# Second attention of a gated cross-attention network: both heads' maxima turned in one tile, masked queries made by ScalarE, order planned anew

## The chip, the cores and the metric

The kernel runs on one core of a Trainium2 chip. The metric is the device time of one execution in microseconds, as the median of several runs. A core has five engines that work side by side, each through its own queue of instructions in order: TensorE (PE, matrix products and transposes, results in PSUM), VectorE (DVE), ScalarE (ACT), GpSimd (POOL) and SyncE (SP, which issues DMAs). Semaphores order them. PSUM has eight banks of 2 KB per partition.

## The reference

For `x` of 8 batches x 256 rows x 256 columns and a context of 8 x 120 x 128:

```text
x = x + tanh(g_xattn[0]) * attention0(layernorm(x), ctx)          # one head
x = x + tanh(g_ffn[0])   * experts(layernorm(x))                  # 8 experts + 4 pass-through, top 2
x = x + tanh(g_xattn[1]) * attention1(layernorm(x), ctx)          # 16 heads of 16
x = x + tanh(g_ffn[1])   * fp8_linear(layernorm(x))               # fp8-rounded weights and inputs
```

The change is in `attention1`:

```text
qh, kh, vh = heads(q @ Wq + bq), heads(k @ Wk + bk), heads(v @ Wv + bv)   # 16 heads of width 16
scores = einsum('bhqd,bhkd->bhqk', qh, kh) / 4
out    = concat(softmax(scores) @ vh) @ Wo + bo
```

A softmax needs each row's maximum taken off before the exponential.

## The kernel before

The program runs in four stages: the first attention with the routing tables (to about 85 us), the blocks of the experts (to about 196 us, and PE then has a branch until 203.9), the second attention (to about 320 us), and the fp8 layer. Within a stage an order written out as text sets each engine's queue: every word is an "atom", a small function that records a few instructions, and each engine takes its own instructions in the order of the words. `ORDER1` is that text for the second attention; `AHEAD` puts the work of batches 0 to 2 that can go early beside the expert blocks. A planner wrote these orders offline; nothing is reordered on the chip.

The second attention works in 16 steps k = (batch b, half ec). A half has 128 of the 256 query columns, which are 8 heads in four "quarters" of 32 partitions (`QR`) with two heads each. Its atoms are:

| atom | engine | what it does (line) |
|---|---|---|
| G.b.c.k | POOL | fetches rows of the experts' results (L1193) |
| cb.b.c | DVE | adds two of them into x (L1203) |
| nf, vf, of; pf | DVE; POOL | moments, variance, offset (L1211 to L1225); power -1/2 (L1220) |
| ap.b.c; tx, xe | ACT; PE, ACT | normalises (L1230); turns x (L1244), copies it out (L1250) |
| q.b, qe.b | PE, ACT | query projection (L1256), out of PSUM with its bias (L1265) |
| gb.b | POOL | adds the output bias to x (L1272) |
| m.k | PE | scores by rows: 8 products of 32 rows, into two PSUM pairs (L1285) |
| r.k.i | DVE | negated maxima over the 120 keys, of pair i, into `mpad` (L1300) |
| p.k | PE | turns `mpad` (L1309) |
| d.k | DVE | puts the turned maxima beside the masked queries (L1319), two instructions |
| w.k | PE | scores by columns, less the maxima, 8 products into two pairs (L1332) |
| e.k.i | ACT | exponential (L1340) |
| o.k, f.k | PE, ACT | product with the values (L1352), copied out (L1359) |
| t.k, c.k, a.k, g.k | PE, DVE, PE, ACT | turned (L1367), divided by the sums (L1373, L1376), turned back (L1386), copied out (L1392) |
| P.b, x.b | PE, DVE | output projection (L1398), added to x (L1405) |
| nb, vb, pb, ob, an, am | DVE, POOL, ACT | the next layer norm (L1230 too), and the largest magnitude (L1412) |

A number after `*` puts that many warm-up matmuls before an atom of PE (L1172). PSUM holds three `pair` tiles of two banks each, taken in turn by m and w (two a step), and two tiles of one bank, `one`, taken in turn by tx, q, p, o, t, a and P. A tile can be written again when whatever read it last has done so.

How a maximum is taken off: `kz` holds, for each quarter, the keys with all rows but one head's set to zero, so a product over 32 rows gives one head's scores. `kq` is the same with a row of ones added in the other head's first row. If the query operand carries the negated maximum in that row, the product comes out with the maximum taken off. `pmask` has two columns, 1 in the rows of head 0 or of head 1 of each quarter. `mpad` is 5 x 128 columns wide; r writes one head's maxima at an offset of 16 and the other's at 0, so that after a transpose for each head and half of the rows (four) each maximum lies in the right row, with zeros elsewhere. d then computes qT x pmask + pm for each of the two heads.

Of the kernel before, what the change touches and what calls it, by code (L numbers as in the profile page):

```python
# [67 lines left out]
ORDER1 = """
m.0 q.2 r.0.0 G.4.0.0 r.0.1 G.4.0.1 m.1 qe.2 cb.3.0 G.4.1.0 p.0 r.1.0 G.4.1.1 d.0 m.2 G.5.0.0
r.1.1 r.2.0 G.5.0.1 p.1*1 d.1 w.0 G.5.1.0 r.2.1 e.0.0 G.5.1.1 cb.3.1 p.2*1 e.0.1 w.1 G.6.0.0 d.2  # L70
o.0 nf.3.0 e.1.0 G.6.0.1 cb.4.0 e.1.1 m.3 G.6.1.0 nf.3.1 f.0 vf.3 o.1 r.3.0 G.6.1.1 t.0 f.1 r.3.1
w.2 pf.3 G.7.0.0 of.3 p.3 c.0 e.2.0 d.3 a.0 G.7.0.1 e.2.1 m.4 cb.4.1 g.0 G.7.1.0 t.1 ap.3.0 r.4.0
o.2 ap.3.1 gb.3 c.1 w.3 f.2 r.4.1 G.7.1.1 a.1 e.3.0 tx.3 nf.4.0 xe.3 m.5 nf.4.1 g.1 vf.4 e.3.1
cb.5.0 pf.4 p.4 q.3 of.4 d.4 ap.4.0 ap.4.1 r.5.0 gb.4 o.3 qe.3 r.5.1 P.0 f.3 nf.5.0 cb.5.1 p.5 x.0
w.4 d.5 t.2 e.4.0 nb.0.0 t.3 c.2 e.4.1 w.5 c.3 a.2 e.5.0 nb.0.1 o.4 vb.0 nf.5.1 pb.0 g.2 m.6 e.5.1
vf.5 pf.5 ob.0 cb.6.0 a.3 f.4 g.3 r.6.0 o.5 an.0.0 an.0.1 P.1 of.5 r.6.1 f.5 ap.5.0 am.0 ap.5.1
p.6 x.1 gb.5 m.7 d.6 tx.4 r.7.0 t.4 xe.4 c.4 q.4 nb.1.0 r.7.1 a.4 qe.4 w.6 cb.6.1 g.4 p.7 nb.1.1
e.6.0 t.5 d.7 e.6.1 m.8 c.5 o.6 r.8.0 a.5 f.6 r.8.1 w.7 g.5 vb.1 p.8 cb.7.0 e.7.0 pb.1 P.2 ob.1
e.7.1 d.8 an.1.0 nf.6.0 o.7 an.1.1 x.2 w.8 nb.2.0 f.7 nb.2.1 t.6 e.8.0 vb.2 t.7 pb.2 c.6 e.8.1 m.9
c.7 ob.2 a.6 r.9.0 an.2.0 o.8 g.6 an.2.1 tx.5 r.9.1 f.8 xe.5 am.1 p.9 q.5 d.9 cb.7.1 w.9 qe.5  # L80
nf.6.1 vf.6 t.8 nf.7.0 pf.6 e.9.0 a.7 c.8 g.7 m.10 of.6 e.9.1 nf.7.1 a.8 vf.7 ap.6.0 r.10.0 pf.7
o.9 g.8 ap.6.1 P.3 of.7 r.10.1 f.9 gb.6 ap.7.0 am.2 ap.7.1 p.10 x.3 gb.7 m.11 d.10 tx.6 nb.3.0 t.9
xe.6 r.11.0 q.6 c.9 r.11.1 a.9 qe.6 w.10 nb.3.1 g.9 vb.3 p.11 pb.3 e.10.0 P.4 d.11 e.10.1 ob.3
an.3.0 o.10 x.4 an.3.1 w.11 nb.4.0 f.10 am.3 t.10 e.11.0 nb.4.1 tx.7 c.10 e.11.1 m.12 vb.4 pb.4
xe.7 o.11 r.12.0 a.10 f.11 r.12.1 m.13 g.10 ob.4 p.12 an.4.0 r.13.0 q.7 an.4.1 d.12 am.4 w.12 qe.7
r.13.1 t.11 e.12.0 p.13 c.11 e.12.1 m.14 d.13 a.11 r.14.0 o.12 g.11 P.5 r.14.1 f.12 t.12 x.5 w.13
c.12 nb.5.0 e.13.0 a.12 p.14 nb.5.1 e.13.1 m.15 d.14 g.12 vb.5 pb.5 r.15.0 o.13 r.15.1 f.13 w.14
ob.5 t.13 e.14.0 p.15 c.13 e.14.1 d.15 a.13 g.13 w.15 an.5.0 an.5.1 o.14 e.15.0 am.5 P.6 f.14
e.15.1 o.15 x.6 nb.6.0 t.14 f.15 c.14 t.15 c.15 a.14 g.14 nb.6.1 a.15 vb.6 g.15 pb.6 P.7*1 ob.6
an.6.0 an.6.1 x.7 nb.7.0 nb.7.1 vb.7 am.6 pb.7 ob.7 an.7.0 an.7.1 am.7  # L90
"""
# [7 lines left out]
def flamingo_gated(ctx: ExitStack, tc: tile.TileContext, a: dict, out: bass.AP):  # L99
    nc = tc.nc  # L100
# [1191 lines left out]
    def at_r1(k, i):  # L1292

        sc = held["m", k][i]

# [4 lines left out]
        nc.vector.tensor_reduce(  # L1300
            m[:, :, :, :, 0], sc[:, :, : 4 * SK].rearrange("p r (c h k) -> p r c h k", c=TB, h=2),
            AX.X, ALU.max, negate=True,
        )

    def at_p1(k, warmed):
        pm = held["p", k] = one(f"pm_{k}", warmed, (P, 2, TB * P))
        for h in range(2):
            for c in range(TB):
                nc.tensor.transpose(  # L1309
                    pm[:, h, c * P : (c + 1) * P], mpad[k % 2][:, (2 * c + h) * P :][:, :P], ident  # L1310
                )

    def at_d1(k):

        b, ec = steps[k]
        pm = held.pop(("p", k))
        turned[k] = att1.tile([P, 2, TB * P], F32, tag="qm", name=f"qm_{k}")
        for h in range(2):
            nc.vector.scalar_tensor_tensor(  # L1319
                turned[k][:, h, :], qT[b][:, ec, :], pmask[:, h : h + 1], pm[:, h, :],  # L1320
                ALU.mult, ALU.add,
            )

# [287 lines left out]
```

## Time and profile before

| what | value |
|---|---|
| median of 3 runs | 346.2 us (346.15 to 348.18) |
| profiled execution | 349.1 us |
| its span, first to last instruction | 347.4 us |
| PE busy | 302.6 us, 87% (weight loads 233.3 us, 67%) |
| DVE busy | 237.7 us, 68% |
| ACT busy | 168.0 us, 48% |
| POOL busy | 117.7 us, 34% |
| mean granted TensorE clock | 0.919 |

The profile has the busy time of each engine, the same in stretches of time, groups of instructions by line (busy time, mean of one, and the idle time just before them with what ended it), and a timeline. The mean of one instruction is from its start to its end. Matmuls overlap in PE's pipeline, so the time that one holds PE is read from its start to the start of the next. The profiled execution has its own time, which is not one of the three runs.

### The profile page before, as it was taken

How to read it: one execution, taken by the hardware profiler on the slowest of the kernel's cores; microseconds unless marked ns; L12 is line 12 of the kernel's file. 1: busy time of each engine (PE TensorE's matmuls, PEld its weight loads, DVE VectorE, ACT ScalarE, POOL GpSimd, SP SyncE). 2: the span in 40 equal slices, each digit the busy share in tenths (PEclk: the TensorE clock that was granted, in tenths of full speed). 3: DMA queues.
4: the chain of work that ended last, by engine and by line, in shares of the span. 5: the costliest groups of instructions: out<-in, count | busy, mean ns of one | idle time of the engine just before them, and what ended most of it. 6: DMA issues, size and time to landing. Idle time of an engine off the chain costs nothing. (4 is left out here: it accounts for less than half of the span.)

```text
span 347.4 us, 6779 instructions
## 1 busy us (share of the span) xinstructions
PE 302.6 (87%) x2284; PEld 233.3 (67%) x2284; DVE 237.7 (68%) x714; ACT 168.0 (48%) x331; POOL 117.7 (34%) x165
## 2 busy tenths in 40 slices
...
GB/s 124 285 277 323 123 124 0 2 0 242 256 219 218 187 217 198 215 252 183 256 260 45 107 37 93 94 30 2 2 0 2 4 0 2 3 0 0 2 60 181
DMA packets 26518, 40.18 MB, mean 116 GB/s; under 512 B 4432, under 2 KB 13744, under 8 KB 26480
## 3 DMA queue, kind: packets, MB, share of 16 engines
...
q14 instruction: 16, 0.13, 0.1%
...
## 5 line engine op out<-in xcount | busy, mean ns | idle before, releaser
L1109 PEld LDWEIGHTS bh<-xbT,w 128*128 128x128 f32 x416 | 50.1, 192 | 2.5 <-DVE xbT L1103 1.1
L1109 PE MATMUL bh<-xbT,w 128*128 128x128 f32 x416 | 50.9, 276 | 0.5 <-DVE xbT L1103 0.5
L1120 PE MATMUL by<-w,hidT 128*128 x208 | 49.0, 379 | 0.0
L1300 DVE TENSOR_REDUCE mpad<-sc 128x8 f32<-128x960 f32 x32 | 36.0, 1150 | 14.5 <-PE sc L1285 14.5
L1103 DVE COPY xbT<-bx 128x256 f32<-128x256 f32 x26 | 11.0, 422 | 47.0 <-PE bx L1101 46.8
L1078 POOL DMA_INDIRECT xb<-rows,from_i x26 | 26.8, 1031 | 47.3 <-PE bx L1101 39.4
L1120 PEld LDWEIGHTS by<-w,hidT 128*128 128x128 f32 x208 | 37.6, 190 | 4.1
L1340 ACT ACTIVATE es<-st 120x1024 f32<-120x1024 f32 x32 | 31.5, 1024 | 14.3 <-PE st L1332 10.3
L1193 POOL DMA_INDIRECT y<-made,back x32 | 32.3, 1010 | 14.1 <-issue 13.6
L1114 ACT ACTIVATE hidT<-bh 128x512 f32<-128x512 f32 x26 | 15.5, 597 | 39.3 <-PE bh L1109 36.6
L1220 POOL TENSOR_TENSOR rsd<-ved,mhalf 128x2 f32<-128x2 f32 x8 | 5.7, 715 | 59.9 <-DVE ved L1216 59.9
L1285 PE MATMUL sc<-kz,qT 32*128 32x240 f32 x256 | 21.2, 404 | 5.0 <-PEq L1460 5.0
L1126 ACT COPY yb<-by 128x256 f32<-128x256 f32 x26 | 9.7, 372 | 32.2 <-PE by L1120 31.8
L1285 PEld LDWEIGHTS sc<-kz,qT 32*128 32x128 f32 x256 | 14.2, 192 | 9.5 <-issue 8.5
L1256 PE MATMUL pq<-xT,wq 128*128 128x256 f32 x64 | 17.3, 418 | 1.8 <-ACT xT L1250 1.8
L1332 PE MATMUL st<-qm,kq 32*120 32x256 f32 x256 | 18.6, 398 | 0.2 <-DMA y<-made,back 0.2
L1265 ACT ACTIVATE qT<-pq,bq 128x256 f32<-128x256 f32 x16 | 6.7, 471 | 22.3 <-PE pq L1256 12.6
L1352 PE MATMUL vo<-es,v 120*32 120x256 f32 x256 | 17.1, 385 | 0.1
L1256 PEld LDWEIGHTS pq<-xT,wq 128*128 128x128 f32 x64 | 12.6, 207 | 5.0 <-ACT xT L1250 2.8
L1398 PE MATMUL po<-wo,cT 128*128 128x256 f32 x64 | 15.7, 388 | 0.0
L1203 DVE SCALAR_TENSOR_TENSOR x<-y,share,x 128x256 f32<-128x256 f32 x32 | 15.3, 477 | 0.6
L1220 POOL TENSOR_TENSOR rsc<-vec,mhalf 128x2 f32<-128x2 f32 x8 | 5.7, 718 | 28.8 <-DVE vec L1216 28.5
...
## 6 DMA issues: line engine op xcount, KB each, us to landing
...
```

The lines of the kernel that those rows point to most:

```text
L1078: nc.gpsimd.indirect_dma_start(out=xb[j % NX].bitcast(I32), out_offset=None, in_=rows, in_offset=bass.IndirectOffsetOnAxis(ap=from_i[:, j ...
L1109: nc.tensor.matmul(ph[:, f, :], w1[j % NW][:, dc, f * P : (f + 1) * P], xbT[j][:, dc, :], start=(dc == 0), stop=(dc == DC - 1),)
L1114: nc.scalar.activation(hidT[j], ph, AF.Silu)
L1120: nc.tensor.matmul(py, hidT[j][:, f, :], w2[:, bass.ds(e, 1), f * D : (f + 1) * D].rearrange("p o d -> p (o d)"), start=(f == 0), stop=(f ...
L1193: nc.gpsimd.indirect_dma_start(out=y.bitcast(I32), out_offset=None, in_=made[:n, :], in_offset=bass.IndirectOffsetOnAxis(ap=back_i[:, b * ...
L1256: nc.tensor.matmul(pq[:, ec, :], wq1[:, dc, ec * P : (ec + 1) * P], xq_[b][:, dc, :], start=(dc == 0), stop=(dc == DC - 1),)
L1285: nc.tensor.matmul(held["m", k][r // 2][:, r % 2, c * 2 * SK : (c + 1) * 2 * SK], qT[b][rows_, ec, c * P : (c + 1) * P], kz[rows_, b, ec, ...
L1300: nc.vector.tensor_reduce(m[:, :, :, :, 0], sc[:, :, : 4 * SK].rearrange("p r (c h k) -> p r c h k", c=TB, h=2), AX.X, ALU.max, negate=True,)
L1332: nc.tensor.matmul(st[r // 2][:SK, r % 2, h * TB * P : (h + 1) * TB * P], kq[rows_, b, ec, h, :], qm[rows_, h, :], start=True, stop=True,)
L1340: nc.scalar.activation(weighed[k][:, 2 * i : 2 * i + 2], held["w", k][i][:SK].rearrange("p r (h t) -> p r h t", h=2), AF.Exp, scale=1.0 / ...
L1352: nc.tensor.matmul(vo[r * QR : (r + 1) * QR, h, :], v1[:, b, ec * HC + 2 * r + h, :], es[:, r, h, :], start=True, stop=True,)
L1398: nc.tensor.matmul(po[:, c, :], cT[b][:, dc, c * P : (c + 1) * P], wo1[:, dc, :], start=(dc == 0), stop=(dc == DC - 1),)
```

## The change

- r writes both heads' maxima of a quarter into one tile of 128 rows and columns for each half of the query rows: column 32r + 16h of `mpad`, now 2 x 128 columns wide. p turns it with two transposes, not four, and its result has half the size.
- After this transpose, the two heads' maxima of a quarter lie in one tile, so d multiplies the turned maxima by the mask and adds queries that are masked already: pm x pmask[1 - h] + qz[h].
- The masked queries `qz` are made by a new atom z.b on ACT, two multiplications of 128 x 512 for each batch, into a new tile with two buffers of 4 KB per partition each.
- For a maximum to land in the other head's row, `kz` has its two heads in exchanged order.
- `wk`, `wv` and `ctxT` (some 8 KB per partition) move from a pool that lives all through the kernel to one of the first attention.
- ORDER1 is written anew, with the z atoms in it and without the warm-ups before p.1 and p.2. `AHEAD`, ORDER and ORDER2 stay.

```diff
 ORDER1 = """
-m.0 q.2 r.0.0 G.4.0.0 r.0.1 G.4.0.1 m.1 qe.2 cb.3.0 G.4.1.0 p.0 r.1.0 G.4.1.1 d.0 m.2 G.5.0.0
-r.1.1 r.2.0 G.5.0.1 p.1*1 d.1 w.0 G.5.1.0 r.2.1 e.0.0 G.5.1.1 cb.3.1 p.2*1 e.0.1 w.1 G.6.0.0 d.2
-o.0 nf.3.0 e.1.0 G.6.0.1 cb.4.0 e.1.1 m.3 G.6.1.0 nf.3.1 f.0 vf.3 o.1 r.3.0 G.6.1.1 t.0 f.1 r.3.1
-w.2 pf.3 G.7.0.0 of.3 p.3 c.0 e.2.0 d.3 a.0 G.7.0.1 e.2.1 m.4 cb.4.1 g.0 G.7.1.0 t.1 ap.3.0 r.4.0
-o.2 ap.3.1 gb.3 c.1 w.3 f.2 r.4.1 G.7.1.1 a.1 e.3.0 tx.3 nf.4.0 xe.3 m.5 nf.4.1 g.1 vf.4 e.3.1
-cb.5.0 pf.4 p.4 q.3 of.4 d.4 ap.4.0 ap.4.1 r.5.0 gb.4 o.3 qe.3 r.5.1 P.0 f.3 nf.5.0 cb.5.1 p.5 x.0
-w.4 d.5 t.2 e.4.0 nb.0.0 t.3 c.2 e.4.1 w.5 c.3 a.2 e.5.0 nb.0.1 o.4 vb.0 nf.5.1 pb.0 g.2 m.6 e.5.1
-vf.5 pf.5 ob.0 cb.6.0 a.3 f.4 g.3 r.6.0 o.5 an.0.0 an.0.1 P.1 of.5 r.6.1 f.5 ap.5.0 am.0 ap.5.1
-p.6 x.1 gb.5 m.7 d.6 tx.4 r.7.0 t.4 xe.4 c.4 q.4 nb.1.0 r.7.1 a.4 qe.4 w.6 cb.6.1 g.4 p.7 nb.1.1
-e.6.0 t.5 d.7 e.6.1 m.8 c.5 o.6 r.8.0 a.5 f.6 r.8.1 w.7 g.5 vb.1 p.8 cb.7.0 e.7.0 pb.1 P.2 ob.1
-e.7.1 d.8 an.1.0 nf.6.0 o.7 an.1.1 x.2 w.8 nb.2.0 f.7 nb.2.1 t.6 e.8.0 vb.2 t.7 pb.2 c.6 e.8.1 m.9
-c.7 ob.2 a.6 r.9.0 an.2.0 o.8 g.6 an.2.1 tx.5 r.9.1 f.8 xe.5 am.1 p.9 q.5 d.9 cb.7.1 w.9 qe.5
...
+m.0 z.0 q.2 z.1 r.0.0 G.4.0.0 r.0.1 G.4.0.1 m.1 qe.2 cb.3.0 G.4.1.0 p.0 cb.3.1 d.0 G.4.1.1 r.1.0
+G.5.0.0 r.1.1 w.0 G.5.0.1 nf.3.0 p.1 e.0.0 nf.3.1 G.5.1.0 d.1 e.0.1 m.2 vf.3 cb.4.0 G.5.1.1 z.2
+o.0 r.2.0 G.6.0.0 f.0 r.2.1 w.1 pf.3 cb.4.1 t.0 e.1.0 G.6.0.1 p.2 of.3 c.0 e.1.1 m.3 G.6.1.0 d.2
+ap.3.0 cb.5.0 o.1 ap.3.1 G.6.1.1 r.3.0 tx.3 f.1 gb.3 xe.3 r.3.1 a.0 w.2 g.0 cb.5.1 G.7.0.0 q.3
+e.2.0 nf.4.0 G.7.0.1 nf.4.1 e.2.1 vf.4 nf.5.0 p.3 G.7.1.0 qe.3 m.4 nf.5.1 d.3 G.7.1.1 o.2 r.4.0
+z.3 t.1 pf.4 r.4.1 f.2 m.5 of.4 c.1 ap.4.0 t.2 ap.4.1 r.5.0 a.1 gb.4 g.1 c.2 w.3 vf.5 r.5.1 pf.5
+a.2 e.3.0 P.0 of.5 cb.6.0 ap.5.0 g.2 cb.6.1 e.3.1 p.4 m.6 x.0 ap.5.1 d.4 gb.5 p.5 r.6.0 o.3 d.5
+w.4 f.3 nb.0.0 t.3 r.6.1 e.4.0 tx.4 e.4.1 c.3 w.5 nb.0.1 xe.4 p.6 vb.0 cb.7.0 e.5.0 pb.0 q.4
+cb.7.1 e.5.1 ob.0 d.6 an.0.0 m.7 qe.4 nf.6.0 a.3 nf.6.1 an.0.1 o.4 g.3 r.7.0 z.4 o.5 vf.6 am.0
+pf.6 f.4 w.6 r.7.1 f.5 t.4 of.6 e.6.0 nf.7.0 p.7 c.4 e.6.1 m.8 d.7 ap.6.0 nf.7.1 a.4 ap.6.1 o.6
+vf.7 r.8.0 pf.7 g.4 tx.5 gb.6 f.6 of.7 r.8.1 w.7 xe.5 ap.7.0 q.5 e.7.0 e.7.1 p.8 m.9 qe.5 d.8 z.5
+o.7 r.9.0 ap.7.1 t.5 r.9.1 gb.7 w.8 f.7 c.5 p.9 e.8.0 P.1 d.9 e.8.1 a.5 x.1 w.9 g.5 nb.1.0 P.2
+nb.1.1 e.9.0 vb.1 pb.1 e.9.1 ob.1 t.6 x.2 an.1.0 m.10 an.1.1 c.6 nb.2.0 a.6 t.7 r.10.0 g.6 tx.6
+c.7 m.11 xe.6 r.10.1 a.7 q.6 r.11.0 g.7 r.11.1 P.3 nb.2.1 qe.6 vb.2 am.1 pb.2 z.6 ob.2 p.10 x.3
+an.2.0 m.12 an.2.1 d.10 o.8 am.2 nb.3.0 o.9 f.8 nb.3.1 t.8 vb.3 r.12.0 f.9 pb.3 p.11 c.8 w.10 d.11
+a.8 e.10.0 r.12.1 t.9 g.8 c.9 w.11 e.10.1 ob.3 a.9 an.3.0 o.10 g.9 e.11.0 P.4 f.10 e.11.1 p.12 x.4
...
-    mpad = [near.tile([P, 5 * P], F32, name=f"mpad_{i}", bufs=1) for i in range(2)]
+    mpad = [near.tile([P, TB * P], F32, name=f"mpad_{i}", bufs=1) for i in range(2)]
...
-            nc.vector.tensor_scalar(kz[:, bs, ec, h, :], src, pmask[:, h : h + 1], None, ALU.mult)
+            nc.vector.tensor_scalar(kz[:, bs, ec, 1 - h, :], src, pmask[:, h : h + 1], None, ALU.mult)
...
-        at = DK + 2 * i * QR
-        m = mpad[k % 2][:, at : at + 4 * P].rearrange("p (c s) -> p c s", c=TB)
-        m = m[:, :, : 2 * (P - DK)].rearrange("p c (h s) -> p c h s", h=2)
-        m = m[:, :, :, : 2 * QR].rearrange("p c h (r s) -> p r c h s", r=2)
+        m = mpad[k % 2].rearrange("p (c i r h s) -> p i r c h s", c=TB, i=2, r=2, h=2)[:, i]
...
     def at_p1(k, warmed):
-        pm = held["p", k] = one(f"pm_{k}", warmed, (P, 2, TB * P))
-        for h in range(2):
-            for c in range(TB):
-                nc.tensor.transpose(
-                    pm[:, h, c * P : (c + 1) * P], mpad[k % 2][:, (2 * c + h) * P :][:, :P], ident
-                )
+        pm = held["p", k] = one(f"pm_{k}", warmed, (P, TB * P))
+        for c in range(TB):
+            cs = slice(c * P, (c + 1) * P)
+            nc.tensor.transpose(pm[:, cs], mpad[k % 2][:, cs], ident)
+
+    def at_z1(b):
+
+        qz[b] = att1.tile([P, 2, DC, TB * P], F32, tag="qz", name=f"qz_{b}")
+        for h in range(2):
+            nc.scalar.mul(qz[b][:, h], qT[b], pmask[:, h : h + 1])
...
-                turned[k][:, h, :], qT[b][:, ec, :], pmask[:, h : h + 1], pm[:, h, :],
+                turned[k][:, h, :], pm, pmask[:, 1 - h : 2 - h], qz[b][:, h, ec, :],
                 ALU.mult, ALU.add,
```

More of the change, by code (lines that the diff above doesn't have):

```diff
@@ L80 @@
-c.7 ob.2 a.6 r.9.0 an.2.0 o.8 g.6 an.2.1 tx.5 r.9.1 f.8 xe.5 am.1 p.9 q.5 d.9 cb.7.1 w.9 qe.5
[L81 to L90, printed above, removed]
+m.0 z.0 q.2 z.1 r.0.0 G.4.0.0 r.0.1 G.4.0.1 m.1 qe.2 cb.3.0 G.4.1.0 p.0 cb.3.1 d.0 G.4.1.1 r.1.0
@@ new lines @@
+c.7 m.11 xe.6 r.10.1 a.7 q.6 r.11.0 g.7 r.11.1 P.3 nb.2.1 qe.6 vb.2 am.1 pb.2 z.6 ob.2 p.10 x.3
+an.2.0 m.12 an.2.1 d.10 o.8 am.2 nb.3.0 o.9 f.8 nb.3.1 t.8 vb.3 r.12.0 f.9 pb.3 p.11 c.8 w.10 d.11
+a.8 e.10.0 r.12.1 t.9 g.8 c.9 w.11 e.10.1 ob.3 a.9 an.3.0 o.10 g.9 e.11.0 P.4 f.10 e.11.1 p.12 x.4
+an.3.1 m.13 d.12 tx.7 nb.4.0 o.11 xe.7 nb.4.1 vb.4 q.7 am.3 pb.4 f.11 r.13.0 ob.4 r.13.1 an.4.0
+w.12 qe.7 p.13 an.4.1 t.10 d.13 e.12.0 c.10 t.11 e.12.1 m.14 am.4 c.11 z.7 a.10 r.14.0 o.12 g.10
+r.14.1 a.11 f.12 w.13 g.11 p.14 e.13.0 P.5 d.14 e.13.1 t.12 x.5 m.15 c.12 nb.5.0 a.12 o.13 r.15.0
@@ L91 @@
+g.12 r.15.1 f.13 w.14 nb.5.1 t.13 e.14.0 vb.5 p.15 pb.5 c.13 e.14.1 d.15 a.13 g.13 ob.5 w.15
+an.5.0 an.5.1 P.6 e.15.0 am.5 e.15.1 o.14 x.6 nb.6.0 o.15 f.14 nb.6.1 t.14 vb.6 f.15 pb.6 c.14
+t.15 ob.6 a.14 c.15 an.6.0 g.14 a.15 an.6.1 g.15 am.6 P.7*1 x.7 nb.7.0 nb.7.1 vb.7 pb.7 ob.7
+an.7.0 an.7.1 am.7
 """
@@ L157, in load_row @@
         engine.dma_start(out=t, in_=a[key].partition_broadcast(t.shape[0]))
-    wk = res.tile([P, 2, D], F32, name="wk")
-    wv = res.tile([P, 2, D], F32, name="wv")
-    ctxT = res.tile([P, B * SK], F32, name="ctxT")
+    wk = att0.tile([P, 2, D], F32, name="wk", bufs=1)
+    wv = att0.tile([P, 2, D], F32, name="wv", bufs=1)
+    ctxT = att0.tile([P, B * SK], F32, name="ctxT", bufs=1)
     def load_kv(t, i, key):
@@ L1158, in flamingo_gated @@
     amax = const.tile([P, B + 1], F32, name="amax")
-    mpad = [near.tile([P, 5 * P], F32, name=f"mpad_{i}", bufs=1) for i in range(2)]
-    xq_, qT, cT, back_rows, rstd, off, mv = {}, {}, {}, {}, {}, {}, {}
+    mpad = [near.tile([P, TB * P], F32, name=f"mpad_{i}", bufs=1) for i in range(2)]
+    xq_, qT, qz, cT, back_rows, rstd, off, mv = {}, {}, {}, {}, {}, {}, {}, {}
     held, turned, weighed, summed, cats = {}, {}, {}, {}, {}
```

4 lines of the change are left out of this document (2 added, 2 removed).

## The prediction

> **What bounds the kernel now.** I read the busy time by stretches first. The change sits in the second attention, which runs from about 204 to 315 us.
>
> ```profile
> core 0: us, PE busy (x) PEld busy (x) DVE busy (x) ACT busy (x) POOL busy (x), PEclk, DMA share, GB/s
> ...
> 215.00:240.00 25.00, 24.50 (x277) 16.27 (x273) 23.44 (x59) 16.68 (x24) 12.46 (x14) 1.00 0.18 51
> 240.00:260.00 20.00, 19.76 (x211) 13.49 (x204) 18.62 (x45) 12.71 (x24) 3.42 (x4) 1.00 0.00 1
> 260.00:280.00 20.00, 19.45 (x182) 14.06 (x182) 16.98 (x45) 12.60 (x23) 5.33 (x6) 1.00 0.01 2
> 280.00:300.00 20.00, 20.00 (x210) 13.90 (x212) 16.48 (x38) 12.26 (x20) 0.69 (x1) 1.00 0.00 1
> ```
>
> PE looks full everywhere. DVE is at 94% (23.44 of 25) and 93% up to 260 us, and at 85% and 82% after it. So there are two bounds, and they change places near 260 us. To see what one piece of PE work really costs, I went to the timeline.
>
> ```profile
> 264.36 0.63 PE L1309 MATMUL pm<-ident,mpad 128*128 128x128 f32 x4 [0.31 <-DVE mpad L1300]
> ...
> 264.83 1.90 PE L1256 MATMUL pq<-xT,wq 128*128 128x256 f32 x8
> 265.03 0.87 DVE L1319 SCALAR_TENSOR_TENSOR qm<-qT,pmask,pm 128x256 f32<-128x256 f32 x2 [0.22 <-PE pm L1309]
> ...
> 266.66 1.14 PE L1332 MATMUL st<-qm,kq 32*120 32x256 f32 x16
> ...
> 267.73 0.66 PE L1367 MATMUL vt<-ident,vs 128*128 128x128 f32 x4
> ...
> 269.92 0.44 PE L1386 MATMUL ct<-ident,cat 128*128 128x128 f32 x2
> ...
> 270.29 1.07 PE L1352 MATMUL vo<-es,v 120*32 120x256 f32 x16
> ...
> 271.29 1.99 PE L1398 MATMUL po<-wo,cT 128*128 128x256 f32 x8
> ```
>
> Durations overlap here; what counts is start to next start. Four transposes (pm) hold PE for 264.83 - 264.36 = 0.47 us, two (ct) for 270.29 - 269.92 = 0.37, vo for 1.00, st for 1.07, pq for 1.83. Over the stage the typical paces are m 1.02, p 0.51, w 1.07, o 1.00, t 0.51, a 0.33 per step, and P 1.83, q 1.83, tx 0.51 per batch: 16 x 4.44 + 8 x 1.83 + 6 x 1.83 + 5 x 0.51 = 99.2 us. The stage takes 110.9 (m.0 starts at 203.9, P.7 ends at 314.8). The other 11.7 us: 2.6 go to m.0 and q.2, which run at half pace after PE's idle branch, the rest is waiting.
>
> ```profile
> L1340 ACT ACTIVATE es<-st 120x1024 f32<-120x1024 f32 x32 | 31.5, 1024 | 14.3 <-PE st L1332 10.3 <-issue 3.9
> L1300 DVE TENSOR_REDUCE mpad<-sc 128x8 f32<-128x960 f32 x27 | 30.4, 1150 | 0.8 <-PE sc L1285 0.8
> L1319 DVE SCALAR_TENSOR_TENSOR qm<-qT,pmask,pm 128x256 f32<-128x256 f32 x29 | 12.6, 474 | 2.2 <-PE pm L1309 2.2
> L1309 PE MATMUL pm<-ident,mpad 128*128 128x128 f32 x56 | 8.8, 280 | 0.7 <-DVE mpad L1300 0.7
> ```
>
> These groups are of the stretch from 215 to 320 us. The maxima (L1300) are the largest DVE row and waited for PE just 0.8 us: DVE is the one that is waited for.
>
> **The change, part by part.** *Two transposes fewer a step.* p drops from four to two, so from 0.51 to about 0.31 (the ct row is the same shape twice): 16 x 0.20 = 3.2 us less PE work, 99.2 to 96.0. Which duration counts matters: the Trainium skill ("TensorE: Matmul & The Clock Gate", Part 4) gives about 275 ns for such a transpose in a kernel, and the L1309 row agrees with a mean of 280. By that, 32 x 0.28 = 9 us would go. The starts, 0.11 us apart inside a group, say the mean is mostly pipeline; I take 3.2.
>
> *ACT makes the masked queries.* z is two multiplications of 128x512 a batch by a column. The nearest row is the same form:
>
> ```profile
> L1063 ACT ACTIVATE qm_w<-wf,s_w 128x512 f32<-128x512 f32 x1 | 0.7, 725 | 0.0
> ```
>
> With about 0.1 us overlap, 1.27 us a batch, 8 x 1.27 = 10.2 us; ACT's queue grows from 62 to 72 us of a 111 us stage. z.0 and z.1 stand ahead of qe.2, where ACT now idles for 9.7 us; z.2 stands ahead of f.0, z.4 ahead of f.4, z.7 ahead of g.10. Behind each I find 1 us or more before PE wants the result. Cost 0; without that cover 1.3 us each for z.4 and z.7, the two with least.
>
> *The combining step d* keeps two DVE instructions of one shape; the PSUM operand changes places. L1203, same operation all from SBUF, takes 478 against 474: 0. *r* writes the same 128x8 with other strides: 0. *Clearing mpad* shrinks (2 x 592 ns for 640 columns, now 256), at 141 us, where DVE is under half busy: 0. *wk, wv, ctxT in another pool*: kz's first write (102 us) now waits also for loads that landed before 70 us: 0. POOL's power pf.3 passes three gathers; gathers go out 1.3 us apart, land in 3.1, and are wanted over 5 us after that: 0.
>
> *The two warm-up matmuls* before p.1 and p.2 (0.4 us each) lay in waits of 1.1 us: 0. What they guard is the granted clock, the column after the engines:
>
> ```profile
> 204.00:209.00 5.00, 5.00 (x24) 3.69 (x24) 3.01 (x4) 0.00 (x0) 3.16 (x4) 0.50 0.19 56
> 209.00:214.00 5.00, 4.50 (x43) 2.65 (x41) 3.61 (x6) 2.12 (x3) 3.96 (x4) 0.99 0.37 105
> ```
>
> It was 0.50 after PE's branch of 4.2 us and stayed up over the waits of 1.1 us. The skill (same page, Part 1) puts the limit at some 3.4 us idle; I expect no wait over 1.5 us. If the clock were lost once, 3.4 us at half pace cost 1.7.
>
> *The new order.* This decides. DVE's total is unchanged, but its queue is not. Paces from the trace: r 1.07, d 0.79 a pair, cb 0.92, nf and nb 0.58, c 0.68, x 0.67, am 0.60, small ones 0.09. Summed along each queue, without waits: DVE to the end of d.k, PE to the start of w.k, which needs d.k.
>
> ```text
> k               3     4     7     9    11    15
> before  DVE  16.5  23.3  42.7  54.9  67.6  87.4
>         PE   16.5  25.1  43.0  54.7  69.9  90.8
> after   DVE  21.7  30.9  44.6  51.9  68.0  87.3
>         PE   19.9  25.8  39.2  48.5  65.3  87.6
> ```
>
> DVE counts from 205.95, PE from 203.9 + 2.6 = 206.5. Before, the two keep step. After, cb.3 to cb.7 and nf.3 to nf.6 (10 and 9 pieces against 8 and 6) stand ahead of d.7: DVE is about 5 us late at w.4 and w.7. Up to there PE's saving is worth nothing, as PE waits for DVE. This is also what the skill's "Perfetto Trace Analysis" (Identifying the Most-Contended Engine) says against the change: matmul busy time is no measure of headroom, LDWEIGHTS busy is. PEld is 65 to 70% in the windows above, DVE 94%. By that rule the gain is 0; by the PE row, where starts follow each other without a gap, it is 3.2. The queue sums say: 0 until about w.7, partly after.
>
> The second half of w.7 also needs the PSUM pair that r.8.0 frees (three pairs in turn). r.8.0 ends at 46.3 in the new DVE queue. Walking the head of both queues by hand gives 0.9 us of DVE idle before that. The same walk of the old queue from r.1.0 (210.47) to d.4 gives 19.5 us, the trace 20.4, so I add 0.8 for small waits: 205.95 + 46.3 + 0.9 + 0.8 = 254.0. w.7 ends 0.8 later, at 254.8; before it ended at 255.45. **-0.65.** What is left for PE after w.7 is 96.0 - 40.3 = 55.7, before 99.2 - 44.0 = 55.2: more, as P.1, P.2 and others now come later. **+0.5.** Waits after w.7 were 314.8 - 255.45 - 55.2 = 4.2. In the new order I walk two more: o.8, o.9 and p.11 follow each other through two one-bank tiles (x.3, d.10, f.9 must free them), and the first half of w.11 waits for r.12.1. Together some 1 to 1.5 over what it had. **+1.2.** Sum: **+1.0 us**. The tail and the FFN keep their order of dependence: 0.
>
> The profiled execution took 349.1 us, 347.4 of it span; the median shown is 2.9 lower. The difference carries over: 346.2 + 1.0 = **347.2 us**. A measurement tells about 1% (3.5 us) from no change, so this counts as the same.
>
> **Rivals.** *A wash* as summed (chance 0.57): 347.2, own range 344.7 to 349.6.
>
> *PE's saving comes through* (0.18): if DVE's waits inside the head vanish and PE is the bound from w.1 on, 346.2 - 3.2 = 343.0, at best half a us less. For it: PE starts follow without a gap from 218 us on. Against it: the table, and DVE at 94%.
>
> *DVE idles in its own head* (0.25): slower. The three pairs make a loop: m.5's second half waits for r.4.0, r.5.0 for m.5, w.3's second half for r.5.0, and so on to d.7. As DVE is the late one there, each us that it idles before d.7 passes whole to the end. In the trace it idled 252.4 - 205.95 - 42.7 = 3.8 us up to d.7; I counted 1.7. The old figure again gives +2.1; the loop closing four times at about 0.5 us of handing over gives 2 more, less what the later waits then absorb: 350.0. It decides from 4.2 us of idle on. For it: d.3 comes at 21.7 against 16.5. Against it: DVE has cb and nf pieces ready in these places.
>
> That transposes are not removed can be left out: the order of PE's queue shows two pm in each step.
>
> **Numbers.** Of the wash nearly all lies within 1%; of the PE case a bit over half is beyond 1% faster (0.11), of the DVE case most beyond 1% slower (0.20), with 0.02 on either side for the wash's edges. Faster 0.13, same 0.65, slower 0.22. The range from 342.7 to 350.6 holds the first two cases with the late clock or uncovered z (1.3 to 1.7), and most of the third.
>
> **What will show it.** pm x2 at about 0.3 us from start to start; z of 0.72 us; DVE over 94% busy from 215 to 255; w.3 starting near 232.5 (before 226.9), w.4 near 238.5 (before 235.8), w.7 within 1.5 us of 254; w.11 near 281; P.7 ending near 316. If w.4 is on time, the table fails; if w.7 starts after 257, the DVE rival is right; if P.7 ends before 313, PE was the bound.

## The result and the profile after

The changed kernel took **349.0 us** (median; 347.2 to 350.2) against 346.8 us for the kernel before on the same chip: a ratio of **1.0051, 95% interval 1.0032 to 1.0070**, so 1.8 us more (1.1 to 2.4). Predicted was +1.0.

Some runs of a kernel are over 1.5% above its fastest; the ratios leave these out, and the one profile of experiment 10 is of such a run. The traces also differ outside the changed stage. The first gather of the experts falls anywhere from 81.0 to 86.3 us, with a granted clock of 0.97 to 0.85 up to 80 us. The end after P.7 takes one of two lengths, about 31.6 or 32.5: 32.5 in both traces of before and in experiment 4, the shorter one in after and in all others. So the two profiled spans, 347.4 before and 347.3 after, are no comparison. I compare what lies between: from the end of PE's branch to the end of P.7. (The branch ends at 203.41 us before and 201.47 after.)

| us | before | before, run again | after |
|---|---|---|---|
| end of the branch to m.0 | 0.47 | 0.47 | 2.40 |
| m.0 to end of w.7 | 51.65 | 51.85 | 50.47 |
| end of w.7 to end of P.7 | 59.37 | 59.37 | 61.36 |
| sum: branch to P.7 | 111.48 | 111.69 | 114.24 |

The sum grows by 2.6 to 2.8. With the end, which is 0.9 shorter in after's trace, that is 1.7 to 1.9. The busy time by stretches, after:

```profile
core 0: us, PE busy (x) PEld busy (x) DVE busy (x) ACT busy (x) POOL busy (x), PEclk, DMA share, GB/s
...
204.00:209.00 5.00, 5.00 (x32) 3.57 (x36) 3.01 (x4) 1.87 (x4) 3.78 (x5) 0.62 0.30 85
209.00:214.00 5.00, 3.42 (x38) 1.99 (x32) 4.62 (x10) 2.73 (x4) 3.78 (x5) 1.00 0.32 98
...
215.00:240.00 25.00, 23.17 (x242) 14.56 (x238) 24.51 (x55) 16.25 (x27) 13.20 (x13) 1.00 0.15 44
240.00:260.00 20.00, 19.81 (x226) 13.19 (x222) 18.14 (x44) 18.27 (x30) 4.16 (x5) 1.00 0.01 2
260.00:280.00 20.00, 19.67 (x177) 13.92 (x173) 17.17 (x44) 11.41 (x19) 2.67 (x4) 1.00 0.01 2
280.00:300.00 20.00, 18.97 (x188) 12.73 (x186) 13.64 (x32) 14.76 (x24) 0.69 (x1) 1.00 0.00 1
```

In the head (215 to 240) DVE went from 94 to 98% and PE fell to 93%: PE waits for DVE there. From 240 to 260 three engines are full at once, PE 99%, ACT 91%, DVE 91%; before, ACT was at 64% there. PE has holes again from 280 to 300.

The groups of 215 to 320 us (busy time, mean ns of one | idle time before, with what ended it):

```profile
L1299 DVE TENSOR_REDUCE mpad<-sc 128x8 f32<-128x960 f32 x28 | 31.4, 1147 | 0.1
...
L1322 DVE SCALAR_TENSOR_TENSOR qm<-pm,pmask,qz 128x256 f32<-128x256 f32 x29 | 12.6, 476 | 3.0 <-PE pm L1308 2.9
...
L1314 ACT ACTIVATE qz<-qT,pmask 128x512 f32<-128x512 f32 x12 | 8.0, 718 | 1.4 <-DVE qm L1322 1.2
...
L1308 PE MATMUL pm<-ident,mpad 128*128 128x128 f32 x28 | 5.7, 284 | 0.1
```

The single prices came out as taken: r with its new strides 1147 ns (1150), d 476 (474), z 718 (725), a transpose 284 in the mean. And on PE's timeline after:

```profile
273.65 0.38 PE L1308 MATMUL pm<-ident,mpad 128*128 128x128 f32 x2
273.96 1.09 PE L1286 MATMUL sc<-kz,qT 32*128 32x240 f32 x16
...
278.18 1.83 PE L1335 MATMUL st<-qm,kq 32*120 32x256 f32 x16
279.94 0.44 PE L1389 MATMUL ct<-ident,cat 128*128 128x128 f32 x2
280.45 0.63 PE L1370 MATMUL vt<-ident,vs 128*128 128x128 f32 x4
281.42 1.14 PE L1335 MATMUL st<-qm,kq 32*120 32x256 f32 x16 [0.34 <-DVE mpad L1299]
```

Two transposes hold PE 273.96 - 273.65 = 0.31 us, as against 0.47 for four. But w.10 (278.18) takes 1.76 to the next start where 1.07 is its pace, t.9 (280.45) 0.97 instead of about 0.5, and w.11 waits in the open: the late place that the prediction named.

What it did not name is at the start of the stage. In the first listing ACT and PE after, in the second ACT and PE before:

```profile
202.37 0.72 ACT L1314 ACTIVATE qz<-qT,pmask 128x512 f32<-128x512 f32 x1 [7.22 <-DMA y<-made,back]
203.00 0.82 ACT L1266 ACTIVATE qT<-pq,bq 128x256 f32<-128x256 f32 x2
...
203.87 1.98 PE L1286 MATMUL sc<-kz,qT 32*128 32x240 f32 x16 [6.67 <-ACT qT L1266]
```

```profile
198.95 0.84 ACT L1265 ACTIVATE qT<-pq,bq 128x256 f32<-128x256 f32 x2 [2.08 <-PE pq L1256]
...
203.88 1.98 PE L1285 MATMUL sc<-kz,qT 32*128 32x240 f32 x16 [4.96 <-PEq L1460]
```

The first half of z.0 stands in ACT's queue ahead of qe.1 (the copy of batch 1's queries out of PSUM, which AHEAD puts beside the experts). z.0 is the first write into the pool `att1`, whose memory held other things until the experts ended; so it waits for all of them, to 202.37, nearly a microsecond after PE's branch ended (201.47). ACT takes nine semaphore waits one after the other for it, from 201.67 to 202.33; the listing names the last releaser only. qe.1 follows at 203.00 instead of before the branch, and m.0 needs the PSUM bank that qe.1 frees. Before, m.0 waits for PE's own branch alone (PEq L1460).

### The profile page after: what moved, and what is told of

It reads as the page before. It is cut to its first block, busy times and chain, and to the rows that moved or that the text cites. A ratio compares the mean times of both kernels' runs of the same rounds, so it can differ in the third digit from the quotient of the medians.

```text
span 347.3 us, 6721 instructions
## 1 busy us (share of the span) xinstructions
PE 298.3 (86%) x2250; PEld 228.2 (66%) x2250; DVE 238.9 (69%) x714; ACT 178.6 (51%) x347; POOL 118.2 (34%) x165
## 5 line engine op out<-in xcount | busy, mean ns | idle before, releaser
L1299 DVE TENSOR_REDUCE mpad<-sc 128x8 f32<-128x960 f32 x32 | 35.9, 1147 | 14.1 <-PE sc L1286 14.0
L1194 POOL DMA_INDIRECT y<-made,back x32 | 32.4, 1012 | 14.1 <-issue 13.5
L1286 PE MATMUL sc<-kz,qT 32*128 32x240 f32 x256 | 19.7, 403 | 6.7 <-ACT qT L1266 6.7
L1335 PE MATMUL st<-qm,kq 32*120 32x256 f32 x256 | 22.0, 402 | 3.2 <-DVE mpad L1299 2.4
L1286 PEld LDWEIGHTS sc<-kz,qT 32*128 32x128 f32 x256 | 13.0, 192 | 10.3 <-ACT qT L1266 7.1
L1335 PEld LDWEIGHTS st<-qm,kq 32*120 32x120 f32 x256 | 12.9, 177 | 9.7 <-issue 4.0
L326 PE MATMUL warm<-every 128*128 128x512 bf16 x44 | 15.5, 502 | 1.1 <-DVE every L232 1.1
L1204 DVE SCALAR_TENSOR_TENSOR x<-y,share,x 128x256 f32<-128x256 f32 x32 | 16.0, 508 | 0.6
L1322 DVE SCALAR_TENSOR_TENSOR qm<-pm,pmask,qz 128x256 f32<-128x256 f32 x32 | 13.9, 476 | 3.4 <-PE pm L1308 3.2
```

What stands on the lines that cost most here:

```text
L1194: nc.gpsimd.indirect_dma_start(out=y.bitcast(I32), out_offset=None, in_=made[:n, :], in_offset=bass.IndirectOffsetOnAxis(ap=back_i[:, b * ...
L1204: nc.vector.scalar_tensor_tensor(x, back_rows.pop((b, c, k)), share[:, b * TB + c, k : k + 1], x, ALU.mult, ALU.add)
L1286: nc.tensor.matmul(held["m", k][r // 2][:, r % 2, c * 2 * SK : (c + 1) * 2 * SK], qT[b][rows_, ec, c * P : (c + 1) * P], kz[rows_, b, ec, ...
L1299: nc.vector.tensor_reduce(m[..., 0], sc[:, :, : 4 * SK].rearrange("p r (c h k) -> p r c h k", c=TB, h=2), AX.X, ALU.max, negate=True,)
L1335: nc.tensor.matmul(st[r // 2][:SK, r % 2, h * TB * P : (h + 1) * TB * P], kq[rows_, b, ec, h, :], qm[rows_, h, :], start=True, stop=True,)
```

## The experiments

Times of kernels are told as ratios to the kernel before on the same chip. Where the trace is compared, the measure is the one above, from the branch's end to P.7's end: 111.5 to 111.7 before, 114.24 after.

**1. z.0 and z.1 behind qe.2.**

```diff
-m.0 z.0 q.2 z.1 r.0.0 ... m.1 qe.2 cb.3.0
+m.0 q.2 r.0.0 ... m.1 qe.2 z.0 z.1 cb.3.0
```

> The changed kernel with z.0 and z.1 moved behind qe.2. Theory A (z.0 is the first instruction that writes the new pool, waits there for PE's branch, and holds up the copy of q.1 behind it on ACT, whose PSUM bank m.0 needs): m.0 starts 0.4 to 0.6 us after PE's branch ends, in place of 2.4; d.0 may wait up to 0.5 us for z.0; the time falls by 1.3 to 2 us, ratio to the kernel before about 1.000. Theory B (all of the loss lies in the new order's waits inside the stage): gap or no gap, the time stays at a ratio of 1.005.

Measured: 349.45 us, ratio 1.0062 (1.0033 to 1.0090). m.0 came 0.47 after the branch, so the hold-up is gone; branch to P.7 is 113.18, 1.06 less than after, not 1.93. About half of the gain went elsewhere: q.2 ran longer at half clock (3.54 us to m.1's start, 2.88 after), and w.1's second half waited 1.07 us for the maxima, not 0.86. The expected ratio of about 1.000 was missed: the median shows nothing of the gain.

**2. qz in a pool that is open already.**

```diff
-        qz[b] = att1.tile([P, 2, DC, TB * P], F32, tag="qz", name=f"qz_{b}")
+        qz[b] = near.tile([P, 2, DC, TB * P], F32, tag="qz", name=f"qz_{b}")
```

> The changed kernel with the masked queries in a pool that is open already in the expert stage, so that z.0 has nothing of the closed pools to wait for; the order is the changed kernel's. Theory A: the wait, not the place in the text, is what costs; m.0 starts 0.4 to 0.6 us after the branch, the stage from m.0 to P.7 stays at 111 to 112 us, the ratio falls to 0.999 to 1.001. Theory B: no change, 1.005. If m.0 is on time in the other run and late here, it is the place on ACT and not the wait.

Measured: 348.37 us, ratio 1.0046 (1.0025 to 1.0068); branch to m.0 0.47, branch to P.7 112.96. On ACT and PE in this kernel:

```profile
198.38 0.84 ACT L1266 ACTIVATE qT<-pq,bq 128x256 f32<-128x256 f32 x2 [2.08 <-PE pq L1257]
199.25 1.33 ACT L1314 ACTIVATE qz<-qT,pmask 128x512 f32<-128x512 f32 x2
...
203.14 1.98 PE L1286 MATMUL sc<-kz,qT 32*128 32x240 f32 x16 [4.80 <-PEq L1463]
```

The text of the order is untouched; only the memory differs. In ACT's queue qe.1 now comes ahead of z.0, z.0 runs before the branch ends, and m.0 waits for the branch alone. Eight of the semaphore waits, for the same semaphores, now stand ahead of the first exponential (208.76 to 209.34 us), which is ACT's first write into `att1` here. So the pool, not the work of z, held m.0 up: it brings both the wait and the place ahead of qe.1. It is worth 114.24 - 112.96 = 1.3 us in the trace. The medians do not confirm this price: 1.3 us less than after would be a ratio of 1.0014, below the interval of this kernel and of experiment 1, and the expected 0.999 to 1.001 was missed. This kernel is the base for experiments 8, 9 and 12.

**3 and 4. Two transposes put back, as dummies,** in steps 0 to 7 or in steps 8 to 15.

```diff
-        for c in range(TB):
+        for h in range(2 if k < 8 else 1):      # the other kernel: k >= 8
+            for c in range(TB):
...
```

> The changed kernel with two more transposes in p in steps 0 to 7, whose result nobody reads: PE's work of before in the head of the stage. Theory A (DVE's queue is the bound up to about w.7): w.7 starts at most 0.4 us later, the ratio is 1.005 to 1.0065. Rival (PE is the bound all through): 8 x 0.2 = 1.6 us later, ratio 1.0097.

> The changed kernel with two more transposes in p in steps 8 to 15, whose result nobody reads. Theory A (PE is the bound after w.7): P.7 ends 1.0 to 1.6 us later, ratio 1.008 to 1.0097. Rival (waits for DVE and for PSUM banks bound this part as well): under 0.5 us, ratio under 1.0065.

Measured, from the start of w.0 to the end of P.7: 104.85 after, 104.86 with the dummies in steps 0 to 7, 105.71 with them in steps 8 to 15 (ratios 1.0105, 1.0064 to 1.0146, and 1.0088, 1.0059 to 1.0117). The pair of step 0 lies ahead of w.0; from p.0 to w.0 it took 1.23 us as against 1.17. So in the first eight steps 8 x 0.2 = 1.6 us of PE work vanish but for 0.07; in the last eight 0.86 of 1.6 shows, less than the 1.0 expected. By the traces, the new order makes use of 0.9 of the 3.2 us that the transposes free. The ratio of the first kernel, of six runs, does not fit this: it is nearer to the rival's 1.0097 than to the 1.005 to 1.0065 of theory A. That PE's saving is worth nothing in the head thus rests on one trace.

**5. The new mathematics in the order of before** (z put between, qz in `near`, warm-ups kept).

```diff
-m.0 q.2 r.0.0 ...
+m.0 z.0 q.2 z.1 r.0.0 ...      # then f.1 z.2, f.3 z.3, e.6.1 z.4, f.9 z.5, xe.7 z.6, f.12 z.7
```

> The order of before with the z atoms put into ACT's idle places, the masked queries in the pool that is open already (as in the second run), and the new transposes: the change without its new order. Theory A (the new order puts DVE's work ahead of the head and takes back what the transposes give): w.7 starts within 0.5 us of where it did, since DVE bounds the head in the old order as well; after w.7 PE gains up to 8 x 0.2 = 1.6 us; ratio to before 0.995 to 0.998. Rival (two transposes fewer are hidden everywhere, or z delays the chain): ratio 1.000 or above.

Measured: **344.17 us, ratio 0.9902 (0.9869 to 0.9934)**, faster than both kernels. m.0 and P.7 in this kernel:

```profile
203.91 1.98 PE L1286 MATMUL sc<-kz,qT 32*128 32x240 f32 x16 [5.02 <-PEq L1463]
...
311.07 1.97 PE L1401 MATMUL po<-wo,cT 128*128 128x256 f32 x8
```

Branch to P.7 is 109.61, 1.9 to 2.1 less than before. The gain lies everywhere: m.0 to w.4 31.17 (31.95 before), w.4 to w.7 18.33 (18.55), w.7 to P.7 59.64 (60.51). I had expected it behind w.7 alone, with w.7 within 0.5 us of its place and a ratio of 0.995 to 0.998; w.7 came 1.0 us earlier. By the ratio the time falls by 3.4 us (2.3 to 4.6), more than this stretch shows. The shorter end after P.7, 31.7 us and not 32.5, would be 0.8 of the difference; the rest stays open.

**6. The new order alone,** with before's mathematics.

```diff
-    (ORDER1 of before)
+    (ORDER1 of after, without its z atoms)
```

> The kernel before with the changed order less its z atoms: four transposes, no masked queries by ACT, m.0 held up by nothing. Theory A: the head is DVE's, so w.3 at 28.5 and w.7 at 50 us after m.0, as in the changed kernel; the rest is longer by 0.9 us, as in the run with more transposes after step 8; ratio to before 1.006 to 1.009. Rival (the new order is neutral, and z is what costs): ratio 0.999 to 1.002.

Measured: 349.33 us, ratio 1.0049 (1.0031 to 1.0068), between the two theories; m.0 and P.7:

```profile
199.56 1.98 PE L1285 MATMUL sc<-kz,qT 32*128 32x240 f32 x16 [5.06 <-PEq L1460]
...
311.13 1.97 PE L1398 MATMUL po<-wo,cT 128*128 128x256 f32 x8
```

Branch to P.7 is 114.02, 2.3 to 2.5 more than before. Together with 5 this settles the sign: the mathematics saves 2, the order costs more than that. With the new mathematics the order's price is larger still, 112.96 (experiment 2) - 109.61 = 3.35, since it also hides the transposes that were saved. By the ratios the two prices are 0.5% and 1.4%, some 1.7 and 5.0 us. The price of the order includes that of its missing warm-ups.

**7. The kernel before, once more,** as a measure of the noise.

> The kernel before, unchanged, for the noise of the comparison and for a second profile of it. Both theories: ratio 1.000 within 0.002; the stage from m.0 to P.7 within 0.7 us of 111.0. If it is not, a difference of that size in the other runs means nothing.

Measured: 347.52 us, ratio 1.0002 (0.9977 to 1.0026); the stretch from branch to P.7 agrees with the first trace of before within 0.2 us.

**8. Less of DVE's work ahead of d.7.** cb.7, nf.6, nf.7 and what hangs on them stand later (3.8 us of DVE).

```diff
-... vb.0 cb.7.0 e.5.0 ... cb.7.1 ... nf.6.0 a.3 nf.6.1 ... nf.7.0 p.7 c.4 ... d.7 ap.6.0 nf.7.1
+... vb.0 e.5.0 ... d.7 ... r.8.1 nf.6.0 nf.6.1 ... d.9 cb.7.0 ... x.1 cb.7.1 ... am.2 nf.7.0 nf.7.1
```

> The changed order with its work for batches 6 and 7 (cb.7, nf.6, nf.7 and what follows them, 4.2 us of DVE) moved from ahead of d.7 to behind r.8.1, d.9, x.1 and d.10, and the masked queries in the open pool. Theory A: d.7 comes 3.8 us earlier in DVE's queue, w.7 starts 2 to 3 us earlier than in the changed kernel and P.7 ends 1.5 to 3 us earlier; ratio to before 0.994 to 1.000. Rival (PSUM tiles and not DVE's queue set w.7): w.7 moves by under 0.7 us, ratio 1.003 to 1.005.

Measured: 353.08 us, ratio 1.0131 (1.0088 to 1.0175), outside both expectations. The busy time about w.4 to w.7, first in experiment 2, then here (columns as in the table of stretches above):

```profile
238.90:254.40 15.50, 15.30 (x181) 10.07 (x178) 15.09 (x40) 13.63 (x23) 3.47 (x4) 1.00 0.01 3
```

```profile
239.90:255.30 15.40, 15.22 (x181) 10.02 (x178) 12.07 (x28) 12.56 (x21) 0.70 (x1) 1.00 0.01 2
```

The expectation of my theory was missed. DVE fell from 97 to 78% busy, but w.4 to w.7 took 14.04 us as against 14.12, so DVE's queue ahead of d.7 was not what held w.7. The pieces came back as waits later: w.7 to P.7 grew from 62.6 to 66.6, with one wait of 1.58 us of a.6 for c.6 on DVE and one of 1.36 of w.10's second half for the maxima; the granted clock fell as well, to 0.83 between 280 and 290 us.

**9. z.4 later on ACT,** in the kernel of experiment 2.

```diff
-... r.7.0 z.4 o.5 vf.6 am.0 pf.6 f.4 w.6 r.7.1 f.5 t.4 of.6 e.6.0 nf.7.0 p.7 c.4 e.6.1 m.8
+... r.7.0 o.5 vf.6 am.0 pf.6 f.4 w.6 r.7.1 f.5 t.4 of.6 e.6.0 nf.7.0 p.7 c.4 e.6.1 z.4 m.8
```

> The changed kernel with qz in the long-lived pool, and z.4 (1.34 us of ACT) moved from ahead of f.4 and f.5 to behind e.6.1. To be read against the kernel with qz in that pool alone, where w.4 to w.7 is 14.12 us and the time from m.0 to P.7 112.49. Theory ACT: between w.5 and w.7 ACT, 91% busy, is what PE waits for (f.4, f.5 behind z.4); then w.4 to w.7 falls by 0.4 to 1.0 us and P.7 ends as much earlier, unless d.8, which needs z.4, comes late. Theory PE: after w.5 PE itself is full, its starts sum to 13.4 of the 14.1 us; then w.4 to w.7 falls by 0.3 us or less. Theory DVE: d.7 sets it, no change (within 0.1). The median moves less than can be told in any case.

Measured: 348.9 us, ratio 1.0038 (1.0016 to 1.0060). All three theories missed: w.4 to w.7 did not fall, it grew, from 14.12 to 15.11. On ACT and on PE, in this kernel:

```profile
251.86 1.33 ACT L1314 ACTIVATE qz<-qT,pmask 128x512 f32<-128x512 f32 x2
253.09 1.08 ACT L1231 ACTIVATE xn<-x,offc,rsc 128x256 f32<-128x256 f32 x2
254.07 0.36 ACT L1395 COPY cT<-ct 128x256 f32<-128x256 f32 x1
```

```profile
252.50 1.07 PE L1355 MATMUL vo<-es,v 120*32 120x256 f32 x16
254.48 0.66 PE L1245 MATMUL pt<-ident,xn 128*128 128x128 f32 x4 [0.92 <-ACT cT L1395]
```

z.4 in its new place pushes g.4 (254.07) back, and tx.5 waits 0.92 us for the one-bank tile that g.4 frees. Where the planner had put z.4 it cost next to nothing: PE's own paces from w.4 to w.7 sum to 13.4 of the 14.1 us. So between w.4 and w.7 PE runs within 0.7 us of its own pace, with ACT so close behind that 1.3 us in the wrong place show at once. The 0.7 us are short waits that can take up some work: the dummies p.6 and p.7 of experiment 3, 0.4 us of PE, made this stretch only 0.09 longer than after's.

**10. Experiment 5 with qz in `att1`.** The edit is that of experiment 2, turned round.

> The new mathematics in the order of before, with the warm-ups kept and z put between, and with qz in the pool att1, as in the changed kernel; it differs from the old-order version measured earlier (344.2 us, ratio 0.990) in this pool alone. Theory (first write into a newly opened pool holds up qe.1): m.0 starts about 2.4 us after the end of PE's branch, not 0.47, and the time from that branch's end to P.7's end grows by 1.0 to 1.5 us over 109.6, as part of the 2 us comes back through less half-clock time; the ratio to before is near 0.993. Rival (the hold-up is absorbed where DVE or PE waits anyway): the gap grows, but P.7 ends within 0.5 us of 109.6 after the branch.

Measured: 345.87 us, ratio 0.9950 (0.9912 to 0.9987). The timeline of ACT in this kernel, and of PE:

```profile
204.59 0.72 ACT L1314 ACTIVATE qz<-qT,pmask 128x512 f32<-128x512 f32 x1 [7.79 <-DMA y<-made,back]
205.22 0.82 ACT L1266 ACTIVATE qT<-pq,bq 128x256 f32<-128x256 f32 x2
```

```profile
206.09 1.98 PE L1286 MATMUL sc<-kz,qT 32*128 32x240 f32 x16 [7.24 <-ACT qT L1266]
208.01 3.78 PE L1257 MATMUL pq<-xT,wq 128*128 128x256 f32 x8
```

The same picture in the other order: m.0 2.73 us after the branch, and branch to P.7 112.40, 2.8 more than in experiment 5. Nothing came back here: q.2 ran at half clock (3.71 us to m.1's start, 3.52 in experiment 5) and m.1 in part (1.34 to the next start, not 1.02), while after had the full clock for some of q.2 already (2.88). The pool holds m.0 up in either order; what that costs in the end differs, and here it is at least seen in the medians: 0.9950 against the 0.9902 of experiment 5 is 0.5%, some 1.7 us. The trace with its 2.8 is of the longest run of this kernel, 349.2 us.

**11. Experiment 5 without the warm-ups before p.1 and p.2.**

```diff
-p.1*1 ... p.2*1
+p.1 ... p.2
```

> The same old-order version with qz in the long-lived pool, without the two warm-up matmuls ahead of p.1 and p.2. Prediction's theory (they lay in PE's waits): from m.0 to P.7 109.1 within 0.3 us. Rival A (they held PE up): up to 0.8 us less. Rival B (they kept the granted clock up): half pace comes back for a few us between 209 and 214 us and the stage is 1 to 2 us longer.

Measured: 347.27 us, ratio 0.9982 (0.9958 to 1.0007); branch to P.7 112.32, 2.7 more than in experiment 5. Rival B is right, and stronger than I put it. PE's timeline without the warm-ups, one stretch of its windows, then PE's timeline with them:

```profile
212.07 0.41 PE L1308 MATMUL pm<-ident,mpad 128*128 128x128 f32 x2 [0.86 <-DVE mpad L1299]
212.98 1.19 PE L1335 MATMUL st<-qm,kq 32*120 32x256 f32 x16 [0.49 <-DMA y<-made,back]
214.90 0.69 PE L1308 MATMUL pm<-ident,mpad 128*128 128x128 f32 x2 [0.72 <-DVE mpad L1299]
215.51 2.08 PE L1335 MATMUL st<-qm,kq 32*120 32x256 f32 x16
217.52 1.94 PE L1355 MATMUL vo<-es,v 120*32 120x256 f32 x16
219.38 1.94 PE L1286 MATMUL sc<-kz,qT 32*128 32x240 f32 x16
```

```profile
214.00:218.00 4.00, 3.28 (x30) 1.71 (x30) 3.90 (x10) 2.31 (x3) 3.06 (x3) 0.54 0.36 102
```

```profile
212.69 0.39 PE L1173 MATMUL pm<-every 128*128 128x512 bf16 x1
213.52 0.44 PE L1308 MATMUL pm<-ident,mpad 128*128 128x128 f32 x2 [0.44 <-DMA y<-made,back]
...
215.65 0.39 PE L1173 MATMUL pm<-every 128*128 128x512 bf16 x1
...
216.80 1.14 PE L1335 MATMUL st<-qm,kq 32*120 32x256 f32 x16
217.87 1.07 PE L1355 MATMUL vo<-es,v 120*32 120x256 f32 x16
```

Without the two matmuls of 0.4 us, w, o and m took 2.0, 1.9 and 1.9 us in a row instead of about 1.1, at a granted clock of 0.54, though no single wait was longer than 0.86 us.

**12. The maxima r.12 earlier on DVE,** in the kernel of experiment 2: am.2, nb.3, vb.3, pb.3 and ob.3 stand behind a.9.

```diff
-... d.10 o.8 am.2 nb.3.0 o.9 f.8 nb.3.1 t.8 vb.3 r.12.0 ... r.12.1 ... a.9 an.3.0
+... d.10 o.8 o.9 f.8 t.8 r.12.0 ... r.12.1 ... a.9 am.2 nb.3.0 nb.3.1 vb.3 pb.3 ob.3 an.3.0
```

> The changed kernel with qz in the long-lived pool, and the DVE pieces am.2, nb.3.0, nb.3.1, vb.3 (with pb.3 of POOL and ob.3) moved from ahead of r.12.0 and r.12.1 to behind a.9, where DVE idles for 3.8 us while P.4 runs. To be read against the kernel with qz in that pool alone: from the start of w.9 to that of w.12 27.81 us there, from w.7 to P.7's end 62.56. Prediction's theory (the later waits, +1.2 us, are w.10's and w.11's on the maxima r.12.0 and r.12.1): r.12.0 starts 1.8 us earlier, w.10 falls from 1.76 to about 1.1 us and the waits at t.9 and w.11 go; w.9 to w.12 falls by 1.0 to 1.5, and P.7 ends as much earlier after w.7. Rival (one-bank tiles): o.8, o.9, p.11 follow each other through the two tiles, so d.11 and d.10 hold w.10 as before and less than 0.4 us goes. Second rival: the time is given back at w.13 to w.15, where DVE is late too; w.9 to w.12 falls, P.7 does not.

Measured: 365.4 us, on a chip where the kernel before takes 365.1 (ratio 0.9991, 0.9953 to 1.0028); against the kernels above, only stretches in which PE has its usual paces can be compared. On PE, and then on ACT:

```profile
292.15 1.14 PE L1335 MATMUL st<-qm,kq 32*120 32x256 f32 x16
293.22 0.44 PE L1389 MATMUL ct<-ident,cat 128*128 128x128 f32 x2
293.50 0.60 PE L1370 MATMUL vt<-ident,vs 128*128 128x128 f32 x4
294.40 1.14 PE L1335 MATMUL st<-qm,kq 32*120 32x256 f32 x16 [0.30 <-DVE mpad L1299]
...
298.87 2.86 PE L1401 MATMUL po<-wo,cT 128*128 128x256 f32 x8 [1.97 <-ACT cT L1395]
```

```profile
297.96 0.60 ACT L1231 ACTIVATE xn<-x,offd,rsd 128x256 f32<-128x256 f32 x1 [2.42 <-DVE offd L1226]
298.47 0.35 ACT L1395 COPY cT<-ct 128x256 f32<-128x256 f32 x1
```

w.10 is back at 1.07 and w.9 to w.11 took 17.71 us instead of 18.70: that part of the later waits was the DVE pieces ahead of r.12, as predicted. The waits at t.9 and w.11 stayed (0.90 to the next start, and 0.30). And I had left an.3.0 ahead of g.9 on ACT: it now waited 2.42 us for ob.3, and P.4 for g.9. Behind that wait the granted clock was 0.73 from 298 to 302 us. From w.9 to P.7 it took 55.65 as against 52.98, so the gain at w.10 was lost with interest. The expectation of a shorter w.9 to w.12 was missed.

## Why the prediction was right, and where its steps were not

The forecast, a wash with a small loss, came out: 1.8 us more where 1.0 was summed. Step by step:

- **Transposes: right.** 0.31 us a pair, 0.2 saved a step; the 284 ns of the row are pipeline. Experiment 5 shows 2 of the 3.2 us in an order that lets them through, z included; so the gain of 0 by the share of the weight loads does not hold there.
- **PE's saving worth nothing until about w.7, partly after: right in size, by the traces.** Experiments 3 and 4 give 0.07 and 0.86 of 1.6 us. The ratio of experiment 3 speaks against the first.
- **DVE as the bound of the head: right to about w.4, not to w.7.** w.3 and w.4 started at 232.1 and 239.0 (predicted 232.5 and 238.5), DVE was at 98% from 215 to 255. From w.4 to w.7 PE is near its own pace. The queue sums leave this open, 39.2 - 25.8 = 13.4 for PE and 44.6 - 30.9 = 13.7 for DVE of the 14.1 us; experiment 8 decides against DVE. I read "late by 5 us" as "still held by DVE"; it was lateness carried along. w.7 was at 253.1 all the same, within the 1.5 us of 254 that I gave, so the rival of idling DVE fell.
- **m.0 to the end of w.7, -0.65; after w.7, +0.5 and +1.2: right.** Experiment 2, which is the change without z.0's hold-up, gives 51.14 to the end of w.7 (-0.5 and -0.7 against the two traces of before) and 61.35 from there (+2.0). w.11 started at 281.4 (near 281), P.7 ended at 315.7 (near 316). That these times of day fit is partly luck: m.0 started at 203.87, as before, because the branch ended 1.94 us earlier and z.0 held m.0 up by 1.93. Counted from m.0, experiment 2 has w.4 at 35.8, w.11 at 78.2 and P.7's end at 112.5, where 34.6, 77.1 and 112.1 were forecast. The wait for r.12 is shown by experiment 12; what share the chain of o.8, o.9 and p.11 has was not measured apart.
- **z.0 and z.1, cost 0: the step whose mechanism failed.** I took the place of z.0 from the words of ORDER1 and priced only its duration. What costs is its wait, as the first write into a new pool, with qe.1 behind it: m.0 is 1.93 us late, and by the traces 1.3 us are lost here (experiment 2), 2.8 in the old order (experiment 10; 1.7 by the ratios). To name what is queued behind z.0 on ACT would have found it.
- **z.4 and z.7, hidden: right for z.4,** with little to spare (experiment 9). z.7 was not tried.
- **Warm-ups, 0: right for the profiled run only.** After's clock stayed at 1.00 from 209 us on. But the reason given, no wait near 3.4 us, was wrong: in the old order waits of 0.3 to 0.9 us in a row lost the clock without them (experiment 11). The Trainium skill has this too, on the page I had cited ("TensorE: Matmul & The Clock Gate", A second HAM failure mode: psum-queue depth-cycling: short idles between groups of matmuls can drop the clock); I used only its rule on single gaps. In the new order experiment 8 lost the clock at this place (w.1's second half and m.2 at half pace from 212.8 us), the kernel of experiment 2 did not, so for after it is a matter of the run. The new order with warm-ups was not tried.

So the sum was +1.05 for the order and the mathematics, where experiment 2 has +1.5 in the trace and 1.6 by its ratio, and nothing for z.0, where the trace has +1.3. The trace of after then stands at +2.8 and its median at +1.8. The end after P.7, 0.9 shorter in after's trace, would close this gap. But for experiment 2 the same count gives +0.5 to +0.7, against 1.6 by its ratio. So how much of the hold-up a run pays in the mean stays open, and that the total came out so near to the forecast is in part luck.

What stays open: which of the new order's moves costs how much. Shown in the traces is that the order, its missing warm-ups included, costs 2.4 us with the old mathematics and 3.35 with the new, that about 2.9 of the latter lies after w.7 (62.56 to P.7's end against 59.64), and that r.12's place is about 1.0 of it. Why the ratios put the latter at 5.0 us is not known; that runs without the warm-ups lose the clock more often would be a cause, and was not tested.
